# A graph-network layer on one core: all source rows gathered by POOL, transposes two groups ahead, softplus ahead of the cutoff's product

## The chip, the core and the metric

The kernel runs on one core of a Trainium2 chip. A core has five engines with instruction streams of their own: TensorE (PE, matmuls and transposes; its weight loads are shown apart as PEld), VectorE (DVE), ScalarE (ACT), GpSimd (POOL) and SyncE (SP). They work on a shared on-chip memory and on PSUM, where PE puts its results, and wait for each other through semaphores. Any of ACT, POOL and SP can issue DMA transfers; the profile shows what an engine's sequencer spends on that as ACTq, POOLq or SPq. The metric is the device time of one execution in microseconds; of several executions the median is given.

## The reference, cut to what matters

There are N = 12500 nodes of 64 features and E = 200000 edges, sorted by their destination node.

```
nodes    = node_state[edges].reshape(num_edges, -1)         # source row and destination row, 128 wide
gates    = ssp(edge_state @ We1 + be1) @ We2 + be2
gates    = gates * (1 - sigmoid(5 * (distance - 3.5)))      # soft cutoff
h        = ssp(nodes @ Wn1 + bn1) @ Wn2 + bn2
messages = h * gates
message_sum = zeros.at[edges[:, 1]].add(messages)           # summed by destination node
new_state   = node_state + ssp(message_sum @ Ws1 + bs1) @ Ws2 + bs2
x = layernorm(x + new_state)                                # ssp(x) = softplus(x) - ln 2
```

All matrices are float32. For each edge the source node's row must be fetched from memory by an index; the destination rows are nearly consecutive, because the edges are sorted.

## The kernel before, in words

**Groups and slots.** The edges are cut into NG = 391 groups of 512 (GE), each of four slots of 128 edges (K = 4; a slot has one edge per partition). The main loop (L632) does one step per group, for i from -1 to 388; the last group is finished after it. Before the loop stands a preparation: the products of all node rows with the lower half of Wn1 and bn1 are written to a table in memory (loop with L591, L593 to L595), because a window of W = 42 consecutive table rows holds all destination rows of half a group.

**One group's way through the engines.** (1) *load*, SP: the edge states (L278, two groups at a time) and two table windows (L286) into the lower part of a weight tile, five groups ahead. (2) *gather*, POOL: the tile xg holds, for each slot, 64 columns for the source rows and 42 for a one-hot matrix of the destination within the window. A slot is gathered by one indirect DMA that POOL issues (L231). Gathers run 14 groups ahead (AHEAD); xg has AHEAD + BEHIND = 19 buffers, so the gathers of group i+14, issued in step i, wait for the scatter of group i-5, which was the last reader of the same buffer. The first 14 groups are gathered before the loop, and the next five meet empty buffers. (3) *onehot*, DVE (L293). (4) *transposes*, PE: the 128 x 106 slots are transposed into a PSUM tile tx (L307; L304 for slots fetched by rows), and *xcopy*, ACT, copies it to the tile xT (L314). tx has two buffers, xT three. (5) *layer1* on PE: a bias matmul (L319), the edge part (L324), and the node part (L330), in which xT meets the weights with the window of the table, so that one product gives source and destination part. (6) *exps* and *logs*, ACT (L341, L344), and *softplus*, DVE (L349), which takes exp and log of ACT and limits the result. (7) *layer2* on PE, from the step after: a bias matmul (L354), the edge part (L361) and the node part (L366) into the PSUM tile gh, of which there are two. (8) *hcut*, DVE (L375): the node part by the cutoff; *message*, DVE (L379): that by the gate. (9) *scatter*, PE (L383): message by one-hot, into a spare piece of the z tile of the group then in layer 1; *window*, DVE (L400): added to the sums of 42 nodes. The scatter of group i-2 stands in step i; in the last twelve steps (CLOSE = 12) it is done one step behind instead of two.

**Slots fetched by rows.** 47 of the 1564 slots are not gathered by POOL. Their rows are fetched one by one: for each of the 128 rows SP or ACT reads the row's address into a register and issues a plain DMA of 256 bytes (*read_rows*, *fetch*, L257). SP does seven such rows a step at the step's start (21 slots, 2688 DMAs), ACT nine (26 slots, 3328 DMAs): three after xcopy, three after the exp, three after the log. A fetched slot has a tile of its own (xr), into which DVE copies its one-hot (L296); the transpose of this slot (L304) waits for its 128 DMAs. The addresses come from a table *rows_i*, loaded by L509 and scaled by L600. One slot of the last group is padding, so POOL gathers 1516.

**What sets the order.** The order of the program is written by hand, and each engine works through its own instructions in that order. A step i issues: load(i+5), SP's rows, gather(i+14), transposes(i+1), xcopy(i+1), ACT's rows, layer1_bias(i+1), layer2_bias(i), scatter(i-2), layer1_edge(i+1), layer1_node(i+1), exps(i+1), ACT's rows, logs(i+1), ACT's rows, window(i-2), layer2(i), hcut(i), message(i), softplus(i+1), onehot(i+3). Waits follow from the data and from the numbers of buffers. Into the steps are laid the parts of 25 node blocks (the update of 512 nodes and the layer norm), each as soon as its sums are complete.

Of the kernel before, what the change touches and what calls it, by code (L numbers as in the profile page):

```python
# [57 lines left out]
P = 128  # L58
# [16 lines left out]
BLOCK_STEPS = ((2, 3, 4, 4, 6, 7, 8, 9, 10, 14), (2, 3, 3, 4, 5, 6, 7, 8, 9, 10), (1, 2, 1, 2, 3))  # L75
ROWS = (7, 9)
READ = 8
ROWS_FROM = -1
READY = (5, 7)
LANDED = 4  # L80
CUTOFF = 5.0
# [22 lines left out]

def slots_by_rows(NG):

    slots = []
    for queue in range(2):
        n = 0
        for g in range(READY[queue], NG - 2):  # L110
            if (g - READY[queue] - ROWS_FROM + 1) * ROWS[queue] >= (n + 1) * P:
                slots.append((queue, g, K - 1 - queue))
                n += 1
    return slots


def row_columns(NG):

    queues = [queue for queue, _, _ in slots_by_rows(NG)]
    return [-(-queues.count(queue) // READ) * READ for queue in range(2)]  # L120


@with_exitstack
def gnn_resnorm_kernel(ctx: ExitStack, tc: tile.TileContext, a: dict, out: bass.AP, E: int):
# [11 lines left out]

    rows_base = nc.sbuf_base + -nc.sbuf_base % 32
    nc.alloc_sbuf_tensor("rows", [P, 4 * P], F32)
    const = ctx.enter_context(tc.tile_pool(name="const", bufs=1))
# [11 lines left out]
    def tx_tile():  # L151
        return psum.tile([P, NB], F32, name="tx")
# [33 lines left out]

    xgs, xrs, eTs = {}, {}, {}
    made = {}
# [12 lines left out]

    slots = slots_by_rows(NG)
    by_rows = {(g, k): n for n, (_, g, k) in enumerate(slots)}
    columns_of = row_columns(NG)
    rows_i = const.tile([P, sum(columns_of)], I32, name="rows_i")
    queues = (nc.sync, nc.scalar)
    firsts = (0, len([1 for queue, _, _ in slots if queue == 0]), len(slots))
    landed = [[tc.alloc_semaphore(f"rows{queue}_{i}") for i in range(LANDED)] for queue in range(2)]
    x_bytes = x.rearrange("(o n) d -> o (n d)", o=1).bitcast(U8)
    table_bytes = table.rearrange("(o n) d -> o (n d)", o=1).bitcast(U8)  # L210

    def arrived(g, k):
        n = by_rows[g, k]
        queue = slots[n][0]
        n -= firsts[queue]
        return landed[queue][n % LANDED], 16 * P * (n // LANDED + 1)

# [3 lines left out]
    def gather(g):  # L221

        xg = loads.tile([P, K, P], F32, name="xg", bufs=AHEAD + BEHIND)
        xgs[g] = xg
        for k in range(K):
            if (g, k) in by_rows:
                continue
            if padding(g, k):
                nc.vector.memset(xg[:, k, :D], 0.0)
                continue  # L230
            note(("gather", g), nc.gpsimd.indirect_dma_start(  # L231
                out=xg[:, k, :D], out_offset=None, in_=x,
                in_offset=bass.IndirectOffsetOnAxis(ap=src_i[:, g, k : k + 1], axis=0)))

    def rows_left(queue):
        return (firsts[queue + 1] - firsts[queue]) * P - fetched[queue]

    def read_rows(i, queue, count):

        count = min(count, rows_left(queue))  # L240
        while i >= ROWS_FROM and len(row_at[queue]) < count:
            q, p = divmod(fetched[queue] + len(row_at[queue]), READ * P)
            assert p % READ == 0
            at = queue * columns_of[0] + q * READ
            row_at[queue] += nc.values_load_multi_w_load_instructions(  # L245
                rows_i[p // READ : p // READ + 1, at : at + READ], engines=[queues[queue].engine], min_val=0,
                max_val=4 * D * (N - 1), skip_runtime_bounds_check_because="src holds rows of x")[1]

    def fetch(i, queue, count):

        for _ in range(min(count, rows_left(queue)) if i >= ROWS_FROM else 0):
            n, r = divmod(fetched[queue], P)
            n += firsts[queue]
            _, g, k = slots[n]
            if r == 0:
                row_tiles[n, "in"], xrs[g, k] = row_tile(queue, n), row_tile(queue, n)
            ins = queues[queue].dma_start(row_tiles[n, "in"][r : r + 1, :D].bitcast(U8),  # L257
                                          x_bytes[:, bass.ds(row_at[queue].pop(0), 4 * D)])
            tc.no_tile_sem_insts.add(ins.ins.name)
            ins.then_inc(arrived(g, k)[0], 16)  # L260
            if r == 0:
                behind(ins, ("rows read", n - 2))
            fetched[queue] += 1

    row_at, row_tiles, fetched = [[], []], {}, [0, 0]

    def row_tile(queue, n):
        return nc.alloc_sbuf_tensor_at(f"xr{queue}_{n % 2}", [P, P], F32,
                                       offset=rows_base + (2 * queue + n % 2) * 4 * P).ap()

# [21 lines left out]
    def onehot(g):  # L292
        last = nc.vector.tensor_tensor(xgs[g][:, :, D:DW], iota, rel[:, g, :].to_broadcast([P, K, W]), OP.is_equal)  # L293
        for k in range(K):
            if (g, k) in by_rows:
                last = nc.vector.tensor_copy(xrs[g, k][:, D:DW], xgs[g][:, k, D:DW])  # L296
                behind(last, ("rows read", by_rows[g, k] - 2))
        note(("onehot", g), last)

    def transposes(g, *needs):  # L300
        tx = tx_tile()[:DW].rearrange("f (k e) -> f k e", k=K)
        for k in range(K):
            if (g, k) in by_rows:
                ins = nc.tensor.transpose(tx[:, k, :], xrs[g, k][:, :DW], ident)  # L304
                note(("rows read", by_rows[g, k]), ins.wait_op(*arrived(g, k), "sem-ge"))
            else:
                ins = nc.tensor.transpose(tx[:, k, :], xgs[g][:, k, :DW], ident)  # L307
            if k == 0:
                behind(ins, *needs)
        xTs[g] = tx  # L310
# [179 lines left out]
    with tc.manual_schedule():  # L490
# [4 lines left out]
        with tc.tile_pool(name="prep", bufs=1) as prep:  # L495
# [11 lines left out]
            for i in range(3):  # L507
                load_x(i)
            nc.sync.dma_start(rows_i, a["rows"])  # L509
            dist = cut.rearrange("p g k -> p (g k)")  # L510
# [75 lines left out]
            for i in range(PARTS):  # L586
# [10 lines left out]
                if i == 1:  # L597
                    nc.vector.tensor_copy(base_i[:1], base_b[:1])
                    nc.vector.tensor_scalar(base_i[32:33], base_b[32:33], float(8 * D), None, OP.mult)
                    nc.vector.tensor_scalar(rows_i, rows_i, float(4 * D), None, OP.mult)  # L600
                    for k in range(2):
                        nc.vector.tensor_copy(be3[:, k, :], rows[:, 0, :])
                    for k in range(K):
                        nc.vector.tensor_copy(row3[:, :, k, :], rows[:, 1:3, :])
                        nc.vector.tensor_copy(rs3[:, k, :], rows[:, 3, :])
# [9 lines left out]
        with tc.tile_pool(name="finish", bufs=1) as finish:  # L615
# [8 lines left out]
            def behind_by(i):  # L624
                close = last - CLOSE
                return [g for g in ([i - 2] if i <= close else []) + ([i - 1] if i >= close else []) if g >= 0]

            for g in range(LOADS - 1):
                load(g)
            for g in range(2):  # L630
                onehot(g)
            for i in range(-1, last - 1):  # L632
                now = parts.pop(i, [])
                early = [part for part in now if part.tensor]
                at(load, i + LOADS)
                read_rows(i, 0, ROWS[0])
                fetch(i, 0, ROWS[0])
                if i >= 0:
                    at(gather, i + AHEAD)
                transposes(i + 1, ("load", i + 1), ("gather", i + 1), ("onehot", i + 1))  # L640
                xcopy(i + 1)
                read_rows(i, 1, ROWS[1])
                fetch(i, 1, ROWS[1] - 6)
                layer1_bias(i + 1)
# [5 lines left out]
                exps(i + 1)  # L650
                fetch(i, 1, 3)
                logs(i + 1)
                fetch(i, 1, 3)
                for g in behind_by(i):
                    window(g)
                at(layer2, i)
                for part in early:
                    part.tensor(tx_tile())
                at(hcut, i)
                at(message, i)  # L660
                softplus(i + 1)
                for part in early:
                    part.others()
                at(onehot, i + 3)
                for part in now:
# [134 lines left out]
def layouts(inputs):  # L800
# [20 lines left out]
    out["src_l"] = lanes(src, 0)  # L821
    rows = []
    for queue, columns in enumerate(row_columns(NG)):
        chosen = [out["src_l"].reshape(P, NG, K)[:, g, k] for q, g, k in slots_by_rows(NG) if q == queue]
        v = padded(np.concatenate(chosen), P * columns, 0).reshape(-1, P, READ)
        rows.append(v.transpose(1, 0, 2).reshape(P, columns))
    out["rows"] = np.ascontiguousarray(np.concatenate(rows, axis=1))
    out["dst_l"] = lanes(dst, dst[-1])
# [44 lines left out]
```

## Time and profile before

| | |
|---|---|
| median of six executions | 2682.14 us (2666.03 to 2702.41) |
| profiled execution | 2686.74 us, span 2685.0 us |
| mean granted clock of PE | 0.811 |
| busy PE, DVE, ACT, POOL | 2253.3, 1052.5, 968.5, 1435.9 us |
| gathers by POOL | 1516, mean 947 ns |
| rows fetched by ACT, by SP | 3328, 2688 of 0.2 KB each |
| first and last xT copy | 144.99 and 2661.49 us |
| last gather ends | 2588.8 us |

Busy times are sums over one engine's instructions; issuing DMAs, registers and semaphores are not counted as busy. The granted clock is the share of full speed that PE was given; a busy PE at a low clock does less. "Idle before, releaser" is the time an engine stood still ahead of an instruction and what ended it, as inferred from semaphore events. The times of the table's last two lines are from the timeline, counted from the span's start.

### The profile page before, as it was taken

Reading aid. Unit: us, or ns where it says so; the run is one execution under the profiler, and the core shown is the slowest. Engines: PE = TensorE matmul, PEld = TensorE weight load, DVE = VectorE, ACT = ScalarE, POOL = GpSimd, SP = SyncE. Lnnn points to the kernel's source line nnn. Section 1 sums busy time; section 2 is a strip of 40 time slices with the busy share of each in tenths; the row PEclk is TensorE's granted clock in tenths of the full one; section 3 lists DMA queues with packets and bytes.
Section 4 is the critical chain, followed back from the end, with each engine's and each line's share of the span. In section 5 each row is a group of like instructions: output and inputs, shape, how many; then the busy total and the mean of one; then the engine's idle time right before and its main releaser. Section 6 shows DMA issues by size and latency. Waiting matters only on the chain.

```text
span 2685.0 us, 47845 instructions
## 1 busy us (share of the span) xinstructions
PE 2253.3 (84%) x11373; PEld 1765.3 (66%) x11373; DVE 1052.5 (39%) x2767; ACT 968.5 (36%) x1318; POOL 1435.9 (53%) x1520
## 2 busy tenths in 40 slices
PE   2488888888988889888888889988888888888898
PEld 1466666666766667666666667766676666666676
DVE  1233333333333333343343443344344444444445
ACT  0133333333333333333333333333333433433444
POOL 7335555555555555555555555555555555555530
PEclk9987877778777787787787787788877987887888
DMA  6221111111111111212111121121112211212210
GB/s 159 79 69 47 49 47 52 48 47 47 47 49 50 49 48 49 53 47 51 49 51 51 50 53 45 49 55 50 51 52 52 56 50 50 56 51 52 56 48 22
DMA packets 150911, 143.53 MB, mean 53 GB/s; under 512 B 51887, under 2 KB 98395, under 8 KB 150626
## 3 DMA queue, kind: packets, MB, share of 16 engines
q1 hardware_dynamic: 94090, 88.26, 11.4%
q0 software_dynamic: 48512, 49.77, 8.2%
q10 hardware_dynamic: 8024, 2.37, 0.4%
q8 instruction: 97, 1.59, 0.2%
q14 instruction: 188, 1.54, 0.2%
HBM read 130.59 MB, written 9.63 MB: 52 GB/s over the span
## 4 chain that ended last, share of the span: by engine, by line
PE 64%; another core or an unknown queue 11%; ACTq 11%; ACT 7%; issue 5%; DVE 1%; DMA 0%; DVEq 0%; SPq 0%
PE z L330 16%; PE gh L366 12%; ACTq L257 10%; PE z L383 10%; PE gh L361 7%; PE tx L307 7%; ACT xT L314 5%; PE z L324 4%; PE gh L354 3%; PE z L319 2%; PE tx L419 1%; PE z L591 1%; ACTq L245 1%; PE tx L450 1%
## 5 line engine op out<-in xcount | busy, mean ns | idle before, releaser
L231 POOL DMA_INDIRECT xg<-in_x,src_i x1516 | 1435.7, 947 | 1152.6 <-issue 358.2
L330 PE MATMUL z<-xT,wns 106*128 106x256 f32 x1564 | 570.4, 500 | 310.0 <-ACT xT L314 297.1
L330 PEld LDWEIGHTS z<-xT,wns 106*128 106x128 f32 x1564 | 360.4, 245 | 469.7 <-ACT xT L314 393.6
L341 ACT ACTIVATE u<-z 128x768 f32<-128x768 f32 x392 | 316.9, 808 | 824.2 <-issue 366.9
L366 PE MATMUL gh<-consts,s 128*128 128x64 f32 x3128 | 499.3, 316 | 0.0
L366 PEld LDWEIGHTS gh<-consts,s 128*128 128x128 f32 x3128 | 495.8, 241 | 0.1
L400 DVE TENSOR_TENSOR sums<-sums,z 64x42 f32 x778 | 153.0, 197 | 833.5 <-issue 626.2
L314 ACT COPY xT<-tx 106x512 f32<-106x512 f32 x391 | 228.6, 585 | 677.1 <-remote 257.3
L375 DVE TENSOR_TENSOR h<-gh,cut 128x256 f32<-128x256 f32 x391 | 166.0, 425 | 642.0 <-PE z L383 235.5
L344 ACT ACTIVATE u<-u,one 128x768 f32<-128x768 f32 x392 | 365.9, 934 | 69.8 <-issue 55.2
L349 DVE SCALAR_TENSOR_TENSOR s<-u,z 128x768 f32<-128x768 f32 x392 | 369.3, 942 | 11.1 <-ACT u L344 9.9
L361 PEld LDWEIGHTS gh<-consts,s 128*128 128x128 f32 x1564 | 304.0, 247 | 71.2 <-DVE s L349 34.1
L383 PEld LDWEIGHTS z<-xg,msg 128*128 128x128 f32 x1556 | 240.8, 222 | 153.4 <-issue 149.1
L361 PE MATMUL gh<-consts,s 128*128 128x128 f32 x1564 | 314.5, 335 | 1.7 <-DVE s L349 1.7
L383 PE MATMUL z<-xg,msg 128*128 128x84 f32 x1556 | 306.8, 327 | 0.9 <-DVE msg L379 0.2
L324 PE MATMUL z<-eT,consts 128*128 128x256 f32 x782 | 296.4, 466 | 0.0
L307 PE MATMUL tx<-consts,xg 128*106 128x128 f32 x1517 | 281.5, 315 | 6.4 <-DMA wns<-table 6.4
L307 PEld LDWEIGHTS tx<-consts,xg 128*106 128x106 f32 x1517 | 220.2, 172 | 11.2 <-issue 8.6
L379 DVE TENSOR_TENSOR msg<-gh,h 128x256 f32<-128x256 f32 x391 | 165.9, 424 | 13.5
L354 PE MATMUL gh<-row,ones 3*128 3x512 bf16 x391 | 170.7, 437 | 0.0
L324 PEld LDWEIGHTS z<-eT,consts 128*128 128x128 f32 x782 | 142.1, 227 | 1.5 <-issue 1.5
L293 DVE TENSOR_TENSOR xg<-consts,rel 128x168 f32<-128x168 f32 x391 | 129.7, 332 | 0.0
(93 smaller groups left out, 614.8 us busy)
## 6 DMA issues: line engine op xcount, KB each, us to landing
xr<-in_x ACTq DMA_DIRECT2D x3328, 0.2 KB
eT<-in_eT SPq DMA_DIRECT2D x195, 256.0 KB
xr<-in_x SPq DMA_DIRECT2D x2688, 0.2 KB
xg<-in_x,src_i POOLq DMA_INDIRECT x1516
wns<-table SPq DMA_DIRECT2D x782, 21.0 KB
table<-tb SPq DMA_DIRECT2D x14, 448.0 KB
sums<-in_xT SPq DMA_DIRECT2D x7, 455.0 KB
y<-in_x SPq DMA_DIRECT2D x24, 128.0 KB
```

The lines of the kernel that those rows point to most:

```text
L231: note(("gather", g), nc.gpsimd.indirect_dma_start(out=xg[:, k, :D], out_offset=None, in_=x, in_offset=bass.IndirectOffsetOnAxis(ap=src_i[ ...
L257: ins = queues[queue].dma_start(row_tiles[n, "in"][r : r + 1, :D].bitcast(U8), x_bytes[:, bass.ds(row_at[queue].pop(0), 4 * D)])
L307: ins = nc.tensor.transpose(tx[:, k, :], xgs[g][:, k, :DW], ident)
L314: note(("xcopy", g), nc.scalar.copy(xT, xTs[g]))
L324: nc.tensor.matmul(zs[g][:, 0, :HE], we1.rearrange("a h d -> a (h d)"), eTs[g], start=False, stop=True, skip_group_check=True)
L330: nc.tensor.matmul(zn, wns[:, g % REST, h, :], xTs[g][:, h], start=True, stop=True, skip_group_check=True)
L341: nc.scalar.activation(us[g][:, part], z_of(g)[:, part], AF.Exp)
L344: nc.scalar.activation(us[g][:, part], us[g][:, part], AF.Ln, bias=one)
L349: nc.vector.scalar_tensor_tensor(ss[g].rearrange("p i t e -> p (i t e)")[:, part], us[g][:, part], BIG, z_of(g)[:, part], OP.min, OP.max)
L361: nc.tensor.matmul(v[:, 0, t], ss[g][:, 0, t, :], we2, start=False, stop=False, skip_group_check=True)
L366: nc.tensor.matmul(ghs[g][:, 1, 2 * t + h, :], ss[g][:, 1 + h, t, :], wn2, start=False, stop=h == 1 and t == 1, skip_group_check=True)
L383: ins = nc.tensor.matmul(sc, msgs[g][:, 2 * t : 2 * t + 2, :].rearrange("p h f -> p (h f)"), xgs[g][:, 2 * t : 2 * t + 2, D:DW], start=t = ...
```

## The change

The slots fetched by rows go: the table of row addresses with its load, its scaling and its host layout, the tiles xr, the semaphores, the register loads, the 6016 row DMAs and the one-hot copies. POOL gathers all 1563 slots that are not padding. The transposes and the xT copy of group i+2, instead of i+1, stand in step i, for all i below last - CLOSE = 378 (`ahead_by`): in step -1 those of the groups 0 and 1, in step 378 none, later those of i+1 as before. Accordingly the one-hot is made a step earlier (three ahead of the loop, then i+4). In the same steps, i below 378, softplus(i+1) stands ahead of hcut(i) and message(i) in DVE's order, and behind the matmuls of the node blocks; from step 378 on it stands behind them as before. The numbers of buffers stay.

```diff
     def gather(g):
         xg = loads.tile([P, K, P], F32, name="xg", bufs=AHEAD + BEHIND)
         xgs[g] = xg
         for k in range(K):
-            if (g, k) in by_rows:
-                continue
             if padding(g, k):
                 nc.vector.memset(xg[:, k, :D], 0.0)
                 continue
...
     def transposes(g, *needs):
         tx = tx_tile()[:DW].rearrange("f (k e) -> f k e", k=K)
         for k in range(K):
-            if (g, k) in by_rows:
-                ins = nc.tensor.transpose(tx[:, k, :], xrs[g, k][:, :DW], ident)
-                note(("rows read", by_rows[g, k]), ins.wait_op(*arrived(g, k), "sem-ge"))
-            else:
-                ins = nc.tensor.transpose(tx[:, k, :], xgs[g][:, k, :DW], ident)
+            ins = nc.tensor.transpose(tx[:, k, :], xgs[g][:, k, :DW], ident)
...
+            def ahead_by(i):
+                return [0, 1] if i < 0 else [i + 2] if i < last - CLOSE else [i + 1] if i > last - CLOSE else []
+
             for g in range(LOADS - 1):
                 load(g)
-            for g in range(2):
+            for g in range(3):
                 onehot(g)
             for i in range(-1, last - 1):
...
                 at(load, i + LOADS)
-                read_rows(i, 0, ROWS[0])
-                fetch(i, 0, ROWS[0])
                 if i >= 0:
                     at(gather, i + AHEAD)
-                transposes(i + 1, ("load", i + 1), ("gather", i + 1), ("onehot", i + 1))
-                xcopy(i + 1)
-                read_rows(i, 1, ROWS[1])
-                fetch(i, 1, ROWS[1] - 6)
+                for g in ahead_by(i):
+                    transposes(g, ("load", g), ("gather", g), ("onehot", g))
+                    xcopy(g)
                 layer1_bias(i + 1)
...
                 exps(i + 1)
-                fetch(i, 1, 3)
                 logs(i + 1)
-                fetch(i, 1, 3)
...
                 for part in early:
                     part.tensor(tx_tile())
+                if i < last - CLOSE:
+                    softplus(i + 1)
                 at(hcut, i)
                 at(message, i)
-                softplus(i + 1)
+                if i >= last - CLOSE:
+                    softplus(i + 1)
                 for part in early:
                     part.others()
-                at(onehot, i + 3)
+                at(onehot, i + 4)
```

More of the change, by code (lines that the diff above doesn't have):

```diff
@@ L75 @@
 BLOCK_STEPS = ((2, 3, 4, 4, 6, 7, 8, 9, 10, 14), (2, 3, 3, 4, 5, 6, 7, 8, 9, 10), (1, 2, 1, 2, 3))
[L76 to L80, printed above, removed]
 CUTOFF = 5.0
@@ L102, in block_steps @@
     return steps
[L105 to L120, printed above, removed]
 @with_exitstack
@@ L135, in gnn_resnorm_kernel @@
     REST = LOADS + 2
-    rows_base = nc.sbuf_base + -nc.sbuf_base % 32
-    nc.alloc_sbuf_tensor("rows", [P, 4 * P], F32)
     const = ctx.enter_context(tc.tile_pool(name="const", bufs=1))
@@ L185, in gnn_resnorm_kernel @@
     wns = const.tile([DW, REST, 2, 2 * D], F32, name="wns")
-    xgs, xrs, eTs = {}, {}, {}
+    xgs, eTs = {}, {}
     made = {}
@@ L200, in behind @@
                                   reason="one place of a step takes its waits")
[L202 to L209, printed above, removed]
-    table_bytes = table.rearrange("(o n) d -> o (n d)", o=1).bitcast(U8)
[L212 to L216, printed above, removed]
+    table_bytes = table.rearrange("(o n) d -> o (n d)", o=1).bitcast(U8)
     def padding(g, k):
@@ L233, in gather @@
                 in_offset=bass.IndirectOffsetOnAxis(ap=src_i[:, g, k : k + 1], axis=0)))
[L235 to L269, printed above, removed]
     bases = {}
@@ L293, in onehot @@
         last = nc.vector.tensor_tensor(xgs[g][:, :, D:DW], iota, rel[:, g, :].to_broadcast([P, K, W]), OP.is_equal)
-        for k in range(K):
-            if (g, k) in by_rows:
-                last = nc.vector.tensor_copy(xrs[g, k][:, D:DW], xgs[g][:, k, D:DW])
-                behind(last, ("rows read", by_rows[g, k] - 2))
         note(("onehot", g), last)
@@ L302, in transposes @@
         for k in range(K):
-            if (g, k) in by_rows:
-                ins = nc.tensor.transpose(tx[:, k, :], xrs[g, k][:, :DW], ident)
-                note(("rows read", by_rows[g, k]), ins.wait_op(*arrived(g, k), "sem-ge"))
-            else:
-                ins = nc.tensor.transpose(tx[:, k, :], xgs[g][:, k, :DW], ident)
+            ins = nc.tensor.transpose(tx[:, k, :], xgs[g][:, k, :DW], ident)
             if k == 0:
@@ L508, in gnn_resnorm_kernel @@
                 load_x(i)
-            nc.sync.dma_start(rows_i, a["rows"])
             dist = cut.rearrange("p g k -> p (g k)")
@@ L599, in gnn_resnorm_kernel @@
                     nc.vector.tensor_scalar(base_i[32:33], base_b[32:33], float(8 * D), None, OP.mult)
-                    nc.vector.tensor_scalar(rows_i, rows_i, float(4 * D), None, OP.mult)
                     for k in range(2):
@@ L821, in layouts @@
     out["src_l"] = lanes(src, 0)
[L822 to L827, printed above, removed]
     out["dst_l"] = lanes(dst, dst[-1])
```

## The prediction

> **What bounds the kernel now.** I read the page's busy shares first, then its chain by engine, the costliest groups, the windows by stage, and last the timeline of single steps.
>
> ```profile
> PE 2253.3 (84%) x11373; PEld 1765.3 (66%) x11373; DVE 1052.5 (39%) x2767; ACT 968.5 (36%) x1318; POOL 1435.9 (53%) x1520
> ...
> PE 64%; another core or an unknown queue 11%; ACTq 11%; ACT 7%; issue 5%; DVE 1%; DMA 0%; DVEq 0%; SPq 0%
> ...
> L231 POOL DMA_INDIRECT xg<-in_x,src_i x1516 | 1435.7, 947 | 1152.6 <-issue 358.2
> L330 PE MATMUL z<-xT,wns 106*128 106x256 f32 x1564 | 570.4, 500 | 310.0 <-ACT xT L314 297.1
> ```
>
> PE looks like the bound, with one stall of 297.1 us at the node matmul L330, and POOL half idle. But the windows show that PE's 84% is a slow PE: in steady work it is busy 174 of 200 us at a granted clock near 0.8; once POOL has gathered everything it is full at clock 1.00.
>
> ```profile
> 2200.00:2400.00 200.00, 174.35 (x898) 135.84 (x897) 86.88 (x233) 77.54 (x108) 112.38 (x120) 0.82 0.20 51
> ...
> 2600.00:2660.00 60.00, 57.98 (x384) 48.02 (x384) 37.93 (x105) 31.70 (x49) 0.00 (x0) 1.00 0.11 31
> ```
>
> Steps there follow each other in 4.09 us, against a mean of 6.45 (from one xT copy to the next), with the same order and the transposes only one group ahead. So the order alone does not make PE stall. What differs is POOL. One step of the loop, in the timeline (start, length, engine, line; idle before and its releaser in brackets):
>
> ```profile
> 1314.49 0.94 POOL L231 DMA_INDIRECT xg<-in_x,src_i  x1 [1.58 <-PE z L383]
> ...
> 1316.93 0.81 ACT L341 ACTIVATE u<-z 128x768 f32<-128x768 f32 x1 [2.17 <-issue]
> ...
> 1317.32 1.00 PE L366 MATMUL gh<-consts,s 128*128 128x64 f32 x8
> ...
> 1318.16 0.60 PE L307 MATMUL tx<-consts,xg 128*106 128x128 f32 x4
> 1318.23 0.94 POOL L231 DMA_INDIRECT xg<-in_x,src_i  x1 [0.30 <-issue]
> ...
> 1319.12 0.68 PE L383 MATMUL z<-xg,msg 128*128 128x84 f32 x4
> ...
> 1320.25 0.42 DVE L375 TENSOR_TENSOR h<-gh,cut 128x256 f32<-128x256 f32 x1 [2.08 <-PE z L383]
> 1320.35 0.58 ACT L314 COPY xT<-tx 106x512 f32<-106x512 f32 x1 [0.92 <-PE z L383]
> ...
> 1320.66 0.94 POOL L231 DMA_INDIRECT xg<-in_x,src_i  x1 [1.48 <-PE z L383]
> ```
>
> POOL's four gathers start at 1314.49 and end at 1319.17. L366 ends at 1318.32 and its reader h starts 1.93 us later; L307 ends at 1318.76, its reader xT starts 1.59 us later; the scatter L383 ends at 1319.80, the gather that waits for it starts 0.86 later. Three waiters on three engines move within 0.41 us, shortly after POOL's run ended. The exp, released by L330 2.4 us into the run, was not late. In the stretch without POOL both readers follow at once:
>
> ```profile
> 2627.53 1.00 PE L366 MATMUL gh<-consts,s 128*128 128x64 f32 x8
> ...
> 2628.57 0.42 DVE L375 TENSOR_TENSOR h<-gh,cut 128x256 f32<-128x256 f32 x1
> ...
> 2629.25 0.60 PE L307 MATMUL tx<-consts,xg 128*106 128x128 f32 x4
> ...
> 2629.88 0.58 ACT L314 COPY xT<-tx 106x512 f32<-106x512 f32 x1 [0.82 <-PE tx L307]
> ```
>
> The longest pieces of the chain tell the same of the first gathers, 76 without a wait from 3.3 to 98.95 us: ACT's table copies wait for PE results that had been ready for tens of us.
>
> ```profile
> 40.95 37.22 another core or an unknown queue
> 78.78 29.50 another core or an unknown queue
> ```
>
> My reading: while POOL issues gathers back to back, PE's signals made later than some 2.5 us after the run's start are held until it ends, about 5.9 us after the start for four gathers and 4.4 for three. POOL's next run waits for the scatter whose signal its own run holds. **So the bound is a lock of step and run**: four gathers spaced 1.249 us (5.0 us) and 1.25 us until the release reaches POOL, 6.25 us. Counted over the POOL rows after the first 76 gathers: 327 runs of four (start to next start: median 6.31 us, mean 6.62, fastest hundredth 6.11), 42 of three (5.53, 5.90), three of two (mean 4.48); 327 x 6.62 + 42 x 5.90 + 3 x 4.48 = 2426 us, from 164.7 to about 2590. The mean stands above the median in steps with a cold PE.
>
> **The change part by part**, against the profiled execution (2686.74 us, span 2685.0; 4.6 above the median 2682.14).
>
> *47 more gathers.* They make all 372 runs fours: 372 x 6.62 = 2463, **+37 us**. If a gather's whole spacing is paid, 47 x 1.249 = +59. If gathers hid in POOL's idle 1152.6 us, 0; the release rows speak against it. I take the middle, +48.
>
> *Row DMAs away.* ACT loses 3328 issues, three taking 0.85 to 1.08 us, over 1000 us of its sequencer; the chain gives ACTq 11% (295 us). But in the step above the exp starts 0.04 us after L330's end and the log 0.18 after the exp; the next xT copy then waits for PE. So beside the lock they cost at most 0.18 a step (67 us), and nothing where the next release waits for POOL's end: 0. The end for the range is -295. SP loses 2688 issues, seven taking 3.93 us of a 6.45 us step; its loads run five groups ahead, so 0. The DVE copies at L296 (47) and loading and scaling the row table lie ahead of the loop or beside 61% idle DVE: 0.
>
> *Transposes and xT copy two ahead.* L330's stall (297.1 us in 211 steps) goes, since its copy is then made a step earlier. Late next is the signal of L366 to h, held as before, then message, scatter and POOL's next run. Two bounds: -297 if nothing else is late, 0 if the lock sets the step. I take 0, nearest to the rows in which h, xT and POOL are released together. PE does the same work; the copy (585 ns) stays ACT's first of a step. At the start a second set of transposes and a copy, about 1.2 us, come before the first step; in the last twelve steps the old distance returns.
>
> *Softplus ahead of cutoff's product and message.* Both come up to 0.94 us later (L349's 942 ns). Their reader, the scatter, stands two steps later, the bias matmul that reuses gh likewise: 0. Softplus no longer waits behind the held h: in the step above the log ended at 1318.86, h started at 1320.25 and message ended at 1321.13, so softplus may start 2.3 us sooner. That helps L361, which waited 1.7 us in all: 0 in the sum, but it loosens PE (second rival). Added onehots ahead of the loop: 0.33 us.
>
> **Sum: 2686.7 + 48 = 2735 us**, with ends 2723 and 2745 for the gathers' price.
>
> The Trainium skill, "Perfetto Trace Analysis", section DMA Optimizations, speaks against the change: where generating descriptors is the limit, balance the DMAs over sync, scalar and GPSIMD; the change does the reverse. "DMA: Bandwidth & Descriptors", section "Issuing engines are not separate DMA queues", speaks for indifference: issuing from several engines saves only a sequencer's time, usually small. By the second the sum would be 2687; the runs of three, 0.72 us shorter in the mean than those of four, side with the first.
>
> **Rivals.**
> *Faster: a warmer PE.* In the loop the granted clock switches between 0.5 and 1.0, and the fall follows stretches of about 3.4 us in which PE had work for less than half; L330's stall makes such stretches. Without it the mean cycle could fall to the median: 372 x 6.31 = 2347, 116 below 2463, so 2723 - 116 = 2607. At the fastest hundredth (6.11) it is 2533. For it: 297 us of stall at one place. Against: the holds remain, and PE cannot do more than one step in a run.
> *Slower: POOL's runs merge.* Today the pause after a run of four is never under 1.2 us, because the stalled PE reaches the scatter only inside the hold. A PE that is no longer stopped at L330 can run forward until a scatter ends less than 2.5 us after a run's start. Then its signal passes at once, POOL goes on without a pause into eight gathers, and everything else is held for 8 x 1.249 + 0.9 = 10.9 us, in which PE completes one step; the second takes another 4.09 or more: 15.0 against 12.6 for the pair, +2.4. One pair in six (31 of 186; the share is my choice, no row gives it) adds 74: 2724 + 74 = 2798; in half of the pairs, 2950. For it: the 76-gather run held PE's signals for 37 us. Against: POOL's buffers free one group a step.
> *It comes to nothing.* The stall's removal gives back the 48 us: 2687, within 1%. One per cent is about what a measurement of this kernel can tell from no change.
>
> **How the numbers follow.** The lock with dearer runs (forecast, 2715 to 2760): 0.40. Merging (2760 to 2950): 0.20. Warmer PE (2530 to 2655): 0.25. Nothing: 0.15. The last case is "same"; so faster 0.25, same 0.15, slower 0.60. The range leaves out a tenth at each side: 2575, about halfway down the faster case, to 2840, about halfway up the merging one; the forecast's own is 2715 to 2760.
>
> **What would show it.** Right: all POOL runs of four, start to start still at 6.2 to 6.7 us in the mean; h and the gather still released together about 5.9 us after a run's start; L330's wait for xT nearly gone but PE's idle time found again elsewhere (at L361, at L383 or at the transposes); ACTq gone from the chain without a shorter span. Merging: runs of eight and gaps below 0.4 us between groups. Warmer PE: clock above 0.9 in the 200 us windows. Wrong would be the whole reading if cycles fell under 5.9 us with four gathers: then the hold was not POOL's run but something of the row DMAs (their issues on SP and ACT run in the same microseconds), and the time could drop below 2500.

## The result and the profile after

The changed kernel takes **2498.81 us (median of 20 runs) against 2684.23 us (46 runs of the kernel before): ratio 0.932, 95% interval 0.930 to 0.934**. Forecast were 2735 us and a range of 2575 to 2840. The change makes the kernel 7% faster here, and this is not the whole result: in sessions described below the kernel before takes 1937 us, and there the same change makes it 3% slower. In what follows ratios are of the mean times of executions without the profiler, and one execution each of rows_kept and eights_old_fifth, more than 1.5% above its kernel's fastest, is left out of median and ratio. First the session of the prediction.

From the page of the changed kernel (busy shares, chain by engine, two of the groups; the node matmul is now L245, the gather L190):

```profile
PE 2064.3 (82%) x11373; PEld 1658.2 (66%) x11373; DVE 1055.2 (42%) x2719; ACT 934.4 (37%) x1318; POOL 1489.9 (59%) x1567
...
PE 76%; issue 10%; another core or an unknown queue 6%; DVE 3%; ACT 3%; DMA 1%; POOL 1%; DVEq 1%; SPq 0%; ACTq 0%; POOLq 0%
...
L190 POOL DMA_INDIRECT xg<-in_x,src_i x1563 | 1489.7, 953 | 913.3 <-issue 409.1
...
L245 PE MATMUL z<-xT,wns 106*128 106x256 f32 x1564 | 486.7, 441 | 0.3 <-issue 0.2
```

PE's stall ahead of the node matmul went from 310.0 to 0.3 us and ACTq left the chain, as the edits should make it. The span fell from 2685.0 to 2506.0 us. In the same 200 us window as before PE does 948 matmuls instead of 898, at a clock of 0.85 instead of 0.82, and POOL 128 gathers instead of 120:

```profile
2200.00:2400.00 200.00, 171.94 (x948) 137.10 (x948) 91.26 (x244) 80.19 (x118) 121.87 (x128) 0.85 0.22 57
```

What became of POOL's runs says where the time went. Counted over POOL's rows: before, 327 runs of four gathers, 42 of three, none longer after the first. After, **164 runs of eight, one of seven and only 42 of four**. The mean cycle of an eight, from start to start, is 12.02 us (160 of the 164 lie between 11.8 and 12.3), of a four 6.28. So 164 x 12.02 + 42 x 6.28 and some 11 us for the seven make 2246 us, against 2426 before: 180 less, and the span is 179 shorter. The whole gain lies in these cycles. Here is one of the eights in the timeline of the changed kernel (start, length, engine, line):

```profile
1308.62 0.94 POOL L190 DMA_INDIRECT xg<-in_x,src_i  x1 [2.18 <-PE gh L281]
...
1309.74 1.07 PE L222 MATMUL tx<-consts,xg 128*106 128x128 f32 x4 [1.13 <-ACT u L256]
...
1310.85 0.58 ACT L229 COPY xT<-tx 106x512 f32<-106x512 f32 x1
...
1311.49 1.15 PE L298 MATMUL z<-xg,msg 128*128 128x84 f32 x4
...
1313.36 1.91 PE L245 MATMUL z<-xT,wns 106*128 106x256 f32 x4
...
1313.71 0.94 POOL L190 DMA_INDIRECT xg<-in_x,src_i  x1 [0.30 <-issue]
...
1315.31 0.81 ACT L256 ACTIVATE u<-z 128x768 f32<-128x768 f32 x1 [3.88 <-issue]
...
1317.46 0.94 POOL L190 DMA_INDIRECT xg<-in_x,src_i  x1 [0.31 <-issue]
...
1317.88 0.68 PE L298 MATMUL z<-xg,msg 128*128 128x84 f32 x4
...
1318.86 1.03 PE L245 MATMUL z<-xT,wns 106*128 106x256 f32 x4
...
1320.20 0.42 DVE L290 TENSOR_TENSOR h<-gh,cut 128x256 f32<-128x256 f32 x1 [2.13 <-PE z L245]
1320.26 0.58 ACT L229 COPY xT<-tx 106x512 f32<-106x512 f32 x1 [3.18 <-PE z L245]
...
1320.58 0.94 POOL L190 DMA_INDIRECT xg<-in_x,src_i  x1 [2.17 <-PE z L245]
```

POOL gathers from 1308.62 to 1318.40 without a pause. In that stretch PE does **two** scatters (L298 at 1311.49 and 1317.88). The readers of PE's later results, h, xT and POOL itself, are again released together, at 1320.2 to 1320.6. In all 164 eights of this trace exactly two scatters lie inside the cycle, in all 42 fours exactly one; that must be so, since each scatter frees the buffer of one group. What makes an eight is when the first of them ends. At the run's start POOL has one buffer; the fifth gather needs the scatter that is still to come. Here that scatter ends at 1312.64, 4.0 us into the run, and the fifth gather starts at 1313.71 without a pause. Over the 164 eights it ends 0.9 to 5.0 us after the run's start, 3.2 in the median; over the 327 fours of before the scatter ended 5.3 us after it in the median, and only 7 times before 3.5 us. The pause at the end of a run (about 2 us for an eight, 1.25 to 1.6 for a four) is paid once for two groups: 8 x 1.249 + 2.03 = 12.02.

So PE's signals aren't held for the whole of a run. Counted over the eights where ACT stood ready: of 89 exps whose matmul ended 2 to 5.5 us into the run 81 started more than 0.3 us late, of 75 with 5.5 to 8 us only 14; and all 78 xT copies whose transposes ended 4 to 10.6 us into it started 11.5 to 11.8 us after its start. What decides which signal passes these counts don't show.

### The profile page after: what moved, and what is told of

Same layout as the page of the kernel before. It is cut to its first block, busy times and chain, and to the rows that moved or that the text cites. A ratio compares the mean times of both kernels' runs of the same rounds, so it can differ in the third digit from the quotient of the medians.

```text
span 2506.0 us, 35116 instructions
## 1 busy us (share of the span) xinstructions
PE 2064.3 (82%) x11373; PEld 1658.2 (66%) x11373; DVE 1055.2 (42%) x2719; ACT 934.4 (37%) x1318; POOL 1489.9 (59%) x1567
## 4 chain that ended last, share of the span: by engine, by line
PE 76%; issue 10%; another core or an unknown queue 6%; DVE 3%; ACT 3%; DMA 1%; POOL 1%; DVEq 1%; SPq 0%; ACTq 0%; POOLq 0%
PE z L245 16%; PE gh L281 14%; PE z L298 11%; PE tx L222 9%; PE z L239 8%; PE gh L276 8%; PE gh L269 4%; PE z L234 3%; ACT u L256 2%; PE tx L334 1%; DVE s L264 1%; PE z L505 1%; ACT u L259 1%; DVE h L290 1%
## 5 line engine op out<-in xcount | busy, mean ns | idle before, releaser
L190 POOL DMA_INDIRECT xg<-in_x,src_i x1563 | 1489.7, 953 | 913.3 <-issue 409.1
L281 PE MATMUL gh<-consts,s 128*128 128x64 f32 x3128 | 445.5, 280 | 72.8 <-issue 71.1
L245 PE MATMUL z<-xT,wns 106*128 106x256 f32 x1564 | 486.7, 441 | 0.3 <-issue 0.2
L281 PEld LDWEIGHTS gh<-consts,s 128*128 128x128 f32 x3128 | 424.3, 205 | 84.3 <-issue 82.6
L229 ACT COPY xT<-tx 106x512 f32<-106x512 f32 x391 | 226.6, 580 | 653.5 <-PE z L245 203.6
L245 PEld LDWEIGHTS z<-xT,wns 106*128 106x128 f32 x1564 | 352.4, 225 | 66.2 <-issue 0.4
L222 PE MATMUL tx<-consts,xg 128*106 128x128 f32 x1564 | 279.3, 309 | 128.7 <-PE gh L281 75.1
L276 PEld LDWEIGHTS gh<-consts,s 128*128 128x128 f32 x1564 | 273.1, 222 | 155.1 <-issue 81.0
L276 PE MATMUL gh<-consts,s 128*128 128x128 f32 x1564 | 279.3, 306 | 101.8 <-issue 64.0
L298 PEld LDWEIGHTS z<-xg,msg 128*128 128x128 f32 x1556 | 240.1, 221 | 154.4 <-issue 148.3
L298 PE MATMUL z<-xg,msg 128*128 128x84 f32 x1556 | 306.1, 327 | 2.2 <-DVE msg L294 1.6
L222 PEld LDWEIGHTS tx<-consts,xg 128*106 128x106 f32 x1564 | 201.6, 156 | 152.3 <-PE gh L281 121.7
```

Source lines behind the costliest of these rows:

```text
L190: note(("gather", g), nc.gpsimd.indirect_dma_start(out=xg[:, k, :D], out_offset=None, in_=x, in_offset=bass.IndirectOffsetOnAxis(ap=src_i[ ...
L229: note(("xcopy", g), nc.scalar.copy(xT, xTs[g]))
L245: nc.tensor.matmul(zn, wns[:, g % REST, h, :], xTs[g][:, h], start=True, stop=True, skip_group_check=True)
L276: nc.tensor.matmul(v[:, 0, t], ss[g][:, 0, t, :], we2, start=False, stop=False, skip_group_check=True)
L281: nc.tensor.matmul(ghs[g][:, 1, 2 * t + h, :], ss[g][:, 1 + h, t, :], wn2, start=False, stop=h == 1 and t == 1, skip_group_check=True)
L298: ins = nc.tensor.matmul(sc, msgs[g][:, 2 * t : 2 * t + 2, :].rearrange("p h f -> p (h f)"), xgs[g][:, 2 * t : 2 * t + 2, D:DW], start=t = ...
```

## The experiments

Theory A: the time is set by POOL's runs, and the new order lets runs of eight come about. Theory B: the row DMAs on ACT's and SP's sequencers were the cost. Theory C (from the second set on): the stalls inside PE's step set the time, and runs of eight are only their sign.

**Each part alone.** Four kernels on one chip, where the kernel before took 2678.53 us.

*pool_only*: the rows go, the order of the step stays.

```diff
             def ahead_by(i):
-                return [0, 1] if i < 0 else [i + 2] if i < last - CLOSE else [i + 1] if i > last - CLOSE else []
+                return [i + 1]
...
-            for g in range(3):
+            for g in range(2):
                 onehot(g)
...
-                if i < last - CLOSE:
-                    softplus(i + 1)
                 at(hcut, i)
                 at(message, i)
-                if i >= last - CLOSE:
-                    softplus(i + 1)
+                softplus(i + 1)
...
-                at(onehot, i + 4)
+                at(onehot, i + 3)
```

> Rows removed, POOL gathers all 1563 slots, but the order of the steps is that of before (transposes one ahead, softplus behind message, onehot three ahead). Theory A (the gain comes from POOL's runs of eight, which the new order alone makes possible): all runs of four, mean cycle near 6.6 us, time 2723 to 2745. Theory B (the gain is the removal of the row DMAs from ACT's and SP's sequencers, 11% ACTq in the chain): 2450 to 2550 us, whatever the run length.

*one_ahead* has of this diff only the transposes' distance and the one-hot's undone, *soft_behind* only softplus's place.

> The changed kernel with the transposes and the xT copy one group ahead again, softplus still first. Theory A: PE stops at the node matmul inside each hold, so it can't reach a second scatter in one run of POOL; runs of four, 2690 to 2745 us. Theory B: 2500 us, as the changed kernel.

> The changed kernel with softplus behind hcut and message again, transposes still two ahead. Theory A, if both moves are needed for runs of eight: softplus waits behind the held h, PE stops at layer 2, runs of four, 2650 to 2730 us; if the transposes alone do it: runs of eight and about 2500 us. Theory B: 2500 us.

*rows_kept* is the kernel before with both moves of the order, rows still fetched by ACT and SP.

> The kernel before, rows fetched by ACT and SP kept, with only the order of the change (transposes two ahead, softplus first below step 378, onehot four ahead). Theory A: runs of eight or seven with 47 gathers less, so 2499 - 47 x 1.249 = 2440 us, down to 2460 if part of it goes to ACT's issues. Theory B: the row DMAs still set the time, 2600 to 2690 us.

Measured (runs and mean cycles counted over each trace's POOL rows; the intervals are 95%):

| kernel | rows | transposes | softplus | us | ratio to before | runs of four (mean us) | runs of eight (mean us) |
|---|---|---|---|---|---|---|---|
| before | yes | one ahead | behind | 2678.53 | 1 | 327 (6.62) | 0 |
| pool_only | no | one ahead | behind | 2652.18 | 0.989 (0.983 to 0.994) | 206 (6.78) | 82 (12.07) |
| one_ahead | no | one ahead | ahead | 2633.36 | 0.980 (0.973 to 0.987) | 204 (6.73) | 83 (12.04) |
| soft_behind | no | two ahead | behind | 2631.62 | 0.983 (0.977 to 0.989) | 217 (6.61) | 77 (11.99) |
| rows_kept | yes | two ahead | ahead | 2612.26 | 0.971 (0.963 to 0.979) | 289 (6.51) | 18 (12.66) |
| changed | no | two ahead | ahead | 2498.81 | 0.932 (0.930 to 0.934) | 42 (6.28) | 164 (12.02) |

(The row of before counts the runs of its own earlier profile; the changed kernel was measured in the first session, and its ratio is to the runs of before there.) Theory B falls as the whole cause: pool_only is 1.1% faster, not 5 to 9%, and one_ahead and soft_behind are far from its 2500; only rows_kept fell into its range, 2600 to 2690. But theory A's numbers fall as well, for pool_only (2723 or more), one_ahead (2690 or more) and rows_kept (2440 to 2460): with 47 more gathers pool_only is faster, so taking the rows away is worth more than the gathers cost, and with the rows kept the new order brings hardly any eights. And the parts do not add: without rows, either move alone gains about 20 us by the medians (each kernel's executions scatter over 11 to 32 us), both together 153, across two sessions whose kernels before differ by 6. The waits of PE show where the time goes. With one move undone, the stall only stands at another place. The longest wait of PE in one_ahead, and in soft_behind:

```profile
PE z L245 <- ACT xT L229: 407.2, 92, 5.8
```

```profile
PE gh L276 <- DVE s L264: 403.2, 93, 6.1
```

407.2 us ahead of the node matmul for the xT copy; or 403.2 us ahead of layer 2's edge part for softplus, which waits behind the held h. With both moves L245 waits 0.3 us, and L276 37.5 us on softplus (101.8 us in all). The first of the two cases expected for soft_behind, that both moves are needed and PE stops at layer 2, is what its trace shows; but 77 of its runs are eights, and its size (2650 to 2730) was too high.

**Forcing the eights.** *eights_old_order* is pool_only with the gathers of two groups issued together in every second step; the first waits for the later scatter.

```diff
-                if i >= 0:
-                    at(gather, i + AHEAD)
+                if i >= 0 and i % 2 == 0:
+                    at(gather, i + AHEAD, ("scatter", i - BEHIND + 1))
+                    at(gather, i + AHEAD + 1)
```

> The kernel pool_only (POOL gathers all, step order of before) with one change: the gathers of two groups are issued together in every second step, the first of them waiting for the later of the two scatters, so that POOL runs in eights whatever the order of the step. Theory A (the length of POOL's runs sets the time, the order of the step only decides which length comes about): nearly all cycles 12.0 us, 186 x 12.02 us = 2236 instead of 2387 for the same groups, so about 2500 us. Theory C (runs of eight are a sign of a PE that stalls less, and not the cause): PE stalls at L245 as in pool_only, cycles of 13 us or more, 2640 us or slower.

With it went the same pairing in the changed kernel (eights_new_order) and two kernels made from the changed one that leave work out; no_gather takes 0 and half_gather 2 for n, and in half_gather the first gather of a group waits for the scatter that frees its buffer:

```diff
-        xg = loads.tile([P, K, P], F32, name="xg", bufs=AHEAD + BEHIND)
-        xgs[g] = xg
-        for k in range(K):
+        if g >= AHEAD + BEHIND:
+            xgs[g] = xgs[g - AHEAD - BEHIND]
+        else:
+            xgs[g] = loads.tile([P, K, P], F32, name="xg", bufs=AHEAD + BEHIND)
+        xg = xgs[g]
+        for k in range(K if g < AHEAD + BEHIND else n):
```

> The changed kernel with the same pairing of gathers. Theory A: the 42 runs of four left (mean 6.28 us) become eights (6.01 a group), 42 x 0.27 = 11 us less: about 2488 us. Theory C: no change or slower from the added wait, 2500 to 2530 us.

> Leaves out the gathers of all groups from 19 on: they use again the rows that lie in the 19 buffers, one-hots, transposes and all the rest stay. Theory A (PE's signals are held while POOL issues gathers): no delay between transposes and xT copy or between layer 2 and h, steps of 4.1 to 4.6 us and a clock above 0.95: 165 + 372 x 4.1 to 4.6 + 94 = 1780 to 1970 us. If the delays came from the order of PE, ACT and DVE among themselves: above 2200 us.

> Leaves out two of the four gathers of every group from 19 on (those slots use the rows already in the buffer); the two others wait for the scatter as before. Theory A, with the hold beginning 2.5 us after a run's start: a run of two is over by then, nothing is held, steps of 4.1 to 4.8 us, 1800 to 2050 us. If any gather holds PE's signals until about 1.2 us after its end, however short the run: POOL's cycle is 2.5 + 1.25 to 2 us, PE's loops of several signals a step wait each time, steps of 5 us or more: above 2100 us.

The answer was another than any of these: on this chip the *kernel before* took **1936.71 us**. eights_old_order took 1995.59 (ratio 1.031, 1.029 to 1.032), eights_new_order 1999.78 (1.032, 1.031 to 1.034), no_gather 1758.12 and half_gather 1759.89 (one execution each, both below what was expected). So the changed kernel itself was run again, as a control.

> The changed kernel itself, as a control for the chip, since on the chip of the last four runs the kernel before took 1937 us and POOL's gathers ran without any pause, while on the chip of the first four it took 2679 us. On a chip that holds PE's signals: 2499 us against 2684, runs of eight. On a chip that does not: POOL alone sets the time, 47 more gathers cost 47 x 1.249 = 59 us, 1937 + 59 = 1996 us, so slower by 3%.

Measured: **1998.84 us against 1936.61, ratio 1.0317 (1.030 to 1.033)**. In its timeline POOL's 1563 gathers run from 3.2 to 1965.8 us with no pause over 0.32 us, and PE's results are not late:

```profile
1302.77 1.00 PE L281 MATMUL gh<-consts,s 128*128 128x64 f32 x8
1303.37 0.94 POOL L190 DMA_INDIRECT xg<-in_x,src_i  x1 [0.30 <-DMA xg<-in_x,src_i]
...
1303.61 0.60 PE L222 MATMUL tx<-consts,xg 128*106 128x128 f32 x4
1304.62 0.95 POOL L190 DMA_INDIRECT xg<-in_x,src_i  x1 [0.30 <-issue]
1304.64 0.57 ACT L229 COPY xT<-tx 106x512 f32<-106x512 f32 x1
```

The transposes L222 end at 1304.21 and the copy L229, next in ACT's order behind the log, starts at 1304.64 in the middle of POOL's endless run; over the stretch from 1200 to 1800 us neither the copy nor the exp nor h ever starts more than 0.3 us after both its engine and its input are ready, while in the first trace of the changed kernel 44% of the copies do. The chain of waits now names POOL and its transfers for a third of the span:

```profile
PE 54%; DMA 21%; POOL 10%; issue 7%; ACT 5%; DVE 4%; POOLq 0%; DVEq 0%; SPq 0%; ACTq 0%
DMA xg<-in_x,src_i 19%; PE z L245 12%; POOL xg L190 10%; PE z L298 8%; PE gh L281 8%; PE tx L222 6%; PE z L239 6%; PE gh L276 4%; PE gh L269 3%; PE z L234 3%; ACT u L256 2%; ACT u L259 2%; DVE s L264 2%; PE z L505 2%; PE tx L334 1%
```

Here POOL alone sets the time, and the change costs what it adds to POOL: 47 x 1.249 = 59 us of the 62 measured. The order of the step gains nothing: with the same pairing the old order took 1995.59 us and the new one 1999.78, and eights_old_order run again beside the changed kernel 1995.52 against its 1998.84.

So there are two kinds of sessions: *held* ones, in which PE's signals are late while POOL gathers, and *free* ones. Each session ran all its kernels and the kernel before on one chip. The sessions with pool_only and with rows_kept_again were held (before: 2678.53 and 2674.90), four others free (1935.71 to 1939.02). The chip numbers 2 and 5 each appear once held and once free; whether a number names the same silicon each time isn't known, so it stays open whether the hold belongs to a chip or to a time. The same kernel shows both: eights_old_order took 1997.53 us in a free session (chip 5), and in a third 1995.44 (chip 2), but 2702.78 in a held one (chip 5). With the hold gone, its granted clock was 0.973 instead of 0.831. And ACT's first table copies, which waited 37.2 us for "remote" in the first gathers of the kernel before, show the hold from the start of a held trace (eights_old_fifth, ACT's waits) and are not there in a free one:

```profile
ACT tb L509 <- remote: 66.9, 3, 37.9
```

*pause_short* was to break POOL's runs:

```diff
             note(("gather", g), nc.gpsimd.indirect_dma_start(...))
+            if k % 2:
+                nc.gpsimd.memset(idle, 0.0)      # one column
```

> The changed kernel with a one-column memset on POOL after every second gather. If the hold needs more than 2.5 us of gathers back to back and this breaks a run: on a chip that holds, runs of two, no late signals, POOL bound at 5.0 us + two pauses of 0.2 to 0.5 us: 165 + 372 x 5.4 to 6.0 + 94 = 2270 to 2490 us. If a pause this short does not end the hold: runs of eight with eight gathers and four memsets, 12.0 + 4 x 0.2 to 0.5 us: 2650 to 2870 us. On a chip that does not hold: 1996 + 782 x 0.2 to 0.5 = 2150 to 2390 us.

In the free session of after_again it took 1998.96 us, and in another 2000.70, the same as without it and not the 2150 or more expected: the memset of 0.11 us fits into POOL's pause of 0.30. half_gather took 1754.21 and 1754.17 us there. Whether it, or a run of only two gathers, ends the hold could not be tried, since these runs fell on free sessions. no_gather met no held session either: that the late results belong to POOL's gathers is read from the held traces alone, in which (in the profiles of both kernels) neither exps nor h start late once POOL has finished.

**The eights in a held session.** The pairing met one at last, beside rows_kept:

> POOL gathers all, step order of before, gathers of two groups issued together. On a chip that holds PE's signals: theory A (run length sets the time), nearly all runs of eight at 12.0 us, about 2500 us against pool_only's 2652; theory C (the stall at the node matmul sets it), 2640 us or slower. On a chip that does not hold: 1996 us.

> The kernel before with only the order of the change, rows still fetched by ACT and SP. On a chip that does not hold PE's signals POOL's 1516 gathers and the tail set the time whatever the order of the step: 1937 us, the same as before, within 0.5%. On a chip that holds: 2615 us against 2679, as in the first call.

rows_kept_again: 2607.44 us against 2674.90, ratio 0.975 (0.969 to 0.981), as in the first session. eights_old_fifth: **2702.78 us, ratio 1.013 (1.002 to 1.023)**, from few executions (2692 to 2728 us). All 186 runs were eights, and the median cycle was 12.08 us; but 78 of 186 took more than 12.3, up to 18.4, and the mean was 13.21. Theory A, that the length of the runs alone sets the time, falls: with the old order forced eights are slower than pool_only's mixture (ratio 0.989 in another session). Part of that may be the pairing itself, since POOL must see two scatters before it starts, where the changed kernel's eights need one; the pairing with the new order, which would tell, met no held session. The timeline shows what the long ones lack:

```profile
1700.13 0.81 ACT L258 ACTIVATE u<-z 128x768 f32<-128x768 f32 x1 [7.36 <-remote]
1700.97 0.94 ACT L261 ACTIVATE u<-u,one 128x768 f32<-128x768 f32 x1
...
1701.31 0.94 POOL L190 DMA_INDIRECT xg<-in_x,src_i  x1 [2.25 <-remote]
...
1702.24 0.57 ACT L231 COPY xT<-tx 106x512 f32<-106x512 f32 x1
...
1702.86 2.07 PE L247 MATMUL z<-xT,wns 106*128 106x256 f32 x4 [5.12 <-ACT xT L231]
...
1705.58 1.81 PE L283 MATMUL gh<-consts,s 128*128 128x64 f32 x8
...
1708.92 1.15 PE L300 MATMUL z<-xg,msg 128*128 128x84 f32 x4
...
1716.69 1.15 PE L300 MATMUL z<-xg,msg 128*128 128x84 f32 x4
...
1718.11 0.95 POOL L190 DMA_INDIRECT xg<-in_x,src_i  x1 [7.10 <-PE z L300]
```

At the release (1700.13) PE has stood for 5.12 us: it needs the xT copy of this very group, which stands behind exp and log in ACT's queue, so PE starts 2.7 us after the release, 1.6 after POOL's start, and cold: its layer 2 takes 1.81 us, where the example before the change showed 1.00 (granted clock 0.50 from 1705 to 1710 us). The node part of layer 1 and layer 2 still stand ahead of the scatter, so the first scatter ends at 1710.07, 8.8 us into the run, and the second at 1717.84, 6.8 us after POOL's eight gathers did (1701.31 + 9.70 = 1711.01); POOL stands for 7.10 us. In the changed kernel's eight above, PE stood for 1.13 us and went on 1.1 us after POOL's start, at first cold as well (its node matmul takes 1.91 us), but with the transposes of a group two steps ahead: the first scatter ends 4.0 us into the run, and the second is done at 1318.56, as POOL ends. So in a held session an eight is cheap if PE has two steps of work at hand, and both moves of the order together give it that. This last sentence is argued, not shown by a run that changes nothing else: it rests on the table above, the waits of PE and these two cycles. Theory C's half, that PE's own stalls matter, is true as well: run length and stalls cannot be taken apart.

No version beats both kernels in both kinds of sessions by these runs. Where PE's signals are held the changed kernel is the fastest measured, where they are free the kernel before, among those that do all the work. rows_kept, which is faster than before by 2.5 to 3% when held, was not met by a free session.

## Why the prediction was wrong, point by point

- **The bound.** That POOL's runs and PE's steps lock through late signals was right for the sessions of the prediction, but not that they are held until a run ends: in its own row the wait of 37.22 us ends at 78.17, in the midst of gathers that go on to 98.95. The long gap ahead of ACT's first copies is the mark that came and went with it. That this lock is not there on every chip or at every time no row of one trace could say.
- **"Everything else is held for 10.9 us, in which PE completes one step; the second takes another 4.09 or more: 15.0 against 12.6 for the pair, +2.4."** This is the step that failed. The merging that the slower rival described did happen, by the kind of condition it named (a scatter that ends early enough in a run), though not by its limit: in 76 of the 164 eights the scatter ended later than 3.5 us into the run and still passed. And it was the gain: an eight takes 12.02 us and holds two whole steps of PE. Against two mean fours of before (13.24; the 12.6 is two medians) that is 1.22 less, times 164 = 200 us. The sign was wrong because I let PE stop at the first held result. With transposes two ahead and softplus early PE has the inputs of two steps; and not every signal in a run is held: in the eight shown the exp at 1315.31 follows L245's end (1315.27) by 0.04 us, 6.7 us into the run. My figure of 2.5 us was read from runs of three and four, where it can't be seen what passes later. The forecast itself, all runs of four at 6.62 us, failed with it: 42 fours are left, at 6.28.
- **"I take 0" for the transposes and for softplus.** Each alone is worth about 20 us without the rows; the two together 153. I priced the moves one at a time, each against the lock, and wrote of softplus that it "loosens PE" without asking what that does together with the other.
- **Row DMAs away: 0.** Too low: pool_only is 26 us faster than before although it gathers 47 slots more, so in a held session the rows cost about 26 + 37 = 63 us, with the forecast's lower price for the gathers, or 85 with the higher (estimates from medians). With the rows kept the new order makes only 18 and 10 eights. Whether the issues on ACT and SP or the runs of three break the rhythm was not separated.
- **47 more gathers: +48, between 37 and 59.** The free sessions show the price bare: 62 us, of which 59 are the gathers' spacing. There the forecast's direction and size (+1.8%, measured +3.2%) would have stood.
- **Faster rival, a warmer PE (2530 to 2655).** The clock rose from 0.811 to 0.859, not above 0.9 (in the trace of before the 108 falls of the granted clock in the loop follow 3.4 us in which PE was busy for 0.50 in the median, 0.02 to 0.67), and fours fell from 6.62 to 6.28, close to the median I had used. But its lower bound was built on fours (6.11 us a group); eights give 6.01, and the measured time lies below it. That the time fell below 2500 is not the sign that the last part of the forecast named for it: the fours kept 6.28 in the mean.
- **Two readings of rows.** The three runs of two average 4.80 us, not 4.48; the sum moves by 1 us. And 4.09 us is the bare step: in the stretch without POOL the steps, with node blocks among them, take 4.66 in the median.
- **Balancing over engines.** The rule of the Trainium skill in "Perfetto Trace Analysis", section DMA Optimizations, that balancing descriptor generation over the engines may help, agrees with the free sessions (59 to 62 us for 47 slots) and not with the held ones, where taking the rows back to POOL gained 1.1% by itself. The statement in "DMA: Bandwidth & Descriptors", section "Issuing engines are not separate DMA queues", that a second issuing engine saves only a sequencer's time, fits the size in the free sessions: POOL, which issues the gathers, is the bound, and its time is what is saved.

## What to carry to other kernels

When signals between two engines come late in batches, price a change by how many steps fit between two batches, and price the edits that remove the stalls of one step together: each alone may only move the stall. Where a rival differs from the forecast only by how much work an engine has left inside a wait, list that work from the new order before choosing its sign. And a wait that no engine's work explains, as "another core or an unknown queue" here, may belong to the session: measure both kernels where it is present and where it is not, before the change is kept.

## What was not expected of the hardware

- One and the same kernel takes 1936 to 1939 us in some sessions and 2675 to 2684 in others. Gathers last 944 to 947 ns in the median, spaced 1.25 us, in traces of both kinds; what differs is how late results of PE are seen by ACT, DVE and POOL: in the first gathers of the kernel before, up to 33 us (table products finished at 45.0 us, copied from 78.20 on). What causes it is open.
- Without late signals the steps of this kernel take 4.09 us in the median when POOL does half of the gathers (half_gather, 1754 to 1760 us) or none after the first 19 groups (no_gather, 1758), with PE busy for 97% of the span at a clock of 0.99, so PE's own limit is near 1755 us, POOL's near 2000, and the rest of a held run, some 500 to 740 us, is waiting and the lower clock that comes with it (0.81 to 0.86 against 0.96 to 0.99).
- In a held session two gathered groups in one run cost 12.0 us, one group 6.0 to 6.6: the pause at a run's end is paid per run, and lasts little longer after eight gathers (about 2.0 us) than after four (1.25 to 1.6).
